# Recommender forward pass on one core: PSUM copies moved to VectorE, more table tiles fetched row by row from SP and ScalarE

## The chip, the cores and the metric

The kernel runs on one core of one Trainium2 chip. The metric is the device time in microseconds (us); the time of a kernel is the median of its runs. In the profile PE is TensorE's matmuls, PEld its weight loads, DVE is VectorE, ACT is ScalarE, POOL is GpSimd and SP is SyncE.

## The reference

A recommender model with attention over a user's history, for B = 16384 users, each with F = 69 item ids; the table `emb` has 100001 rows of E = 96 floats.

```python
u = emb[batch_user]                        # B x 69 x 96
ql = emb[batch_label[:, 0]]                # B x 96
q = broadcast(ql)
z = concatenate([q, u, q - u, q * u])      # B x 69 x 384
h = dice(z @ W1 + b1)                      # 64 wide
att = (h @ W2 + b2) @ W3 + b3              # one weight per item
pre = where(batch_user < ITEM_NUM, u * att, 0)
pooled = einsum('gf,bfe->bge', window, pre)   # 10 groups of items
x = concatenate([pooled, ql])
h = dice(bn(x @ Wf1 + bf1)); h = dice(bn(h @ Wf2 + bf2))
return h @ Wf3 + bf3
```

The items of a user fall into ten groups, and `dice(x) = (alpha * (1 - p) + p) * x` with `p = sigmoid(x)`. Everything is float32.

## The kernel before

**Tiling.** The users are cut into 32 blocks of 512. Of the 69 items of a block, the first 64 make 64 "main" chunks (8 users x 64 items each) and the last 5 make 5 "tail" chunks (512 users, one item each). A chunk is 512 rows of the table, fetched as 4 tiles of 128 rows. There are 32 x 69 = 2208 chunks, and two chunks make one step: 1104 steps, with up to 8 tiles per step.

**How a tile is fetched.** Most tiles are gathered by GpSimd with one indirect DMA of 128 rows (`gather`, L266) into the buffer `u` of the step. Some tiles, always the fourth of a chunk (`SLOT = 3`), are instead fetched row by row: 128 plain DMAs of one row (384 bytes) each, issued from SP's or ScalarE's own queue (L301, in `Singles.fetch`), into one of a few buffers of a tensor called `ring`. The byte offset of each row comes from a register; a register load (L286, in `Singles.load`) fetches the offsets of up to 32 rows from the tile `offsets`. `SP_CHUNKS` and `ACT_CHUNKS` list which chunks have such a tile: before, 109 tiles from SP (one every ten steps, in a ring of 4 buffers) and 136 from ScalarE (one every eight steps, in a ring of 3). SP has nothing else to do but loads and stores, so it runs ahead until its ring is full. ScalarE's rows are dealt out over the steps by the table `turn`: 16 rows per step in three pieces, one ahead of the step's fetch, one between its two chunks and one after it (`scalar_rows`), among ScalarE's other work.

**What a step does.** `fetch` (L359 on) takes for each of its two chunks a PSUM buffer `ptr` (two in all), transposes the four tiles into it on TensorE (L325), has VectorE multiply it by the query to give `quT` (L377, L384 for tail chunks), and has ScalarE copy it to `uT` (L386). `hidden` runs two steps later: four accumulating products per chunk pair into `ph` (L399, L403; two PSUM buffers), then on ScalarE a sigmoid (L405) and a scaled copy (L406), then on VectorE the product `y` (L407). `attend_rows` and `spread`, once per four steps, turn `y` into attention weights `rw` (L414, ScalarE's copy L416, L431, VectorE's L436). `pool` runs seven steps after the fetch: it multiplies the rows in `u` and `ring` by `rw` into `acc` (L325 again, since both go through the helper `read_rows`), and VectorE copies the sums to `pooled` (L470). After that the `u` buffer is free again; the pool of `u` has 14 buffers. For each block `head_gather`, `head_turn` (VectorE's copy L340) and `head_rows` (ScalarE's L349) prepare the query, and `top_steps` computes the dense layers (L502, with ScalarE's pair L483 and L484, called the dice pair below).

**What sets the order.** The order is written out by hand: `plan` lists the work of each of the 1104 steps, and each engine executes its own instructions in that order, waiting on semaphores. A tile of SP's list is placed in the plan six steps ahead of its use; SP may issue it earlier than that. A tile of ScalarE's list for step `m // 2` is dealt out over the `ACT_STEPS` steps that end three steps ahead of its use:

```python
for k in range(ACT_STEPS):
    turn.setdefault(m // 2 - 2 - ACT_STEPS + k, []).append((s, k * ACT_ROWS, min(P, (k + 1) * ACT_ROWS)))
```

Within a step the order is: tail work of step i - 3, `hidden` of step i - 2, `pool` of step i - 7, `fetch` of step i, then work of the blocks.

Of the kernel before, what the change touches and what calls it, by code (L numbers as in the profile page):

```python
# [19 lines left out]
B, F, E, G = 16384, 69, 96, 10  # L20
# [28 lines left out]

ROW_BYTES = 4 * E  # L50
SLOT = 3
SP_CHUNKS = [2 * (10 * s + 8) + 1 for s in range(109)]
SP_RING = 4
ACT_CHUNKS = [2 * (8 * s + 11) for s in range(136)]
ACT_RING = 3
ACT_ROWS = 16
ACT_STEPS = -(-P // ACT_ROWS)
SINGLES = SP_CHUNKS + ACT_CHUNKS
NSB = (len(SINGLES) + P - 1) // P
# [3 lines left out]
def chunk_of(c):  # L63

    n, k = divmod(c, NCH)
    if n == NBLK - 1 and k >= EARLY:
        k = NMAIN + k - EARLY if k < EARLY + NTAIL else k - NTAIL
    return n, k
# [47 lines left out]
def rec_kernel(  # L116
# [12 lines left out]
    nc = tc.nc  # L129
# [1 line left out]

    const = ctx.enter_context(tc.tile_pool(name="const", bufs=1))
    ipool = ctx.enter_context(tc.tile_pool(name="ipool", bufs=2))
    upool = ctx.enter_context(tc.tile_pool(name="upool", bufs=14))
    tpool = ctx.enter_context(tc.tile_pool(name="tpool", bufs=4))
    ypool = ctx.enter_context(tc.tile_pool(name="ypool", bufs=6))
    rpool = ctx.enter_context(tc.tile_pool(name="rpool", bufs=2))
# [3 lines left out]
    def by_field(ap):  # L141

        return ap.rearrange("e (s o) -> e s o", o=1).to_broadcast([ap.shape[0], NS, FM])
# [121 lines left out]
    def gather(table, dst, index):  # L265
        nc.gpsimd.indirect_dma_start(  # L266
            out=dst,
            out_offset=None,
            in_=table,
            in_offset=bass.IndirectOffsetOnAxis(ap=index, axis=0),  # L270
        )
# [3 lines left out]
    class Singles:  # L275
# [19 lines left out]
        def fetch(self, s, start, stop):  # L295

            b, k = self.buffers[s % len(self.buffers)], s % NSEM
            for r in range(start, stop):
                if r % self.group == 0:
                    self.load(s, r)  # L300
                d = self.engine.dma_start(  # L301
                    out=ring[r : r + 1, b], in_=row_bytes[:, bass.ds(self.values[r], ROW_BYTES)]
                ).then_inc(self.sems[k], 16)
                tc.no_tile_sem_insts.add(d.ins.name)
                tc.declare_no_dep(d.ins, group=f"ring{b}", reason="a buffer's readers have waited for its rows")
                fresh.setdefault(b, []).append(d.ins)
            if stop == P:
                for ins in fresh.pop(b):
                    tc.add_to_no_dep_group(f"ring{b}", ins)
                self.given[k] += 16 * P  # L310
                places[self.chunks[s]] = b, self.sems[k], self.given[k]
# [3 lines left out]
    def single(c, t):  # L315
        return places.get(c) if t == SLOT else None

    def wait_for_single(c, t):
        if single(c, t):
            nc.tensor.wait_ge(*single(c, t)[1:])  # L320

    def read_rows(op, out, u, c, t, other, **how):

        at = single(c, t)
        ins = op(out, ring[:, at[0]].bitcast(F32) if at else u[:, 4 * (c % 2) + t, :], other, **how)  # L325
        if at:
            tc.declare_no_dep(ins.ins, group=f"ring{at[0]}", reason="waited for by semaphore")
# [25 lines left out]
    def room(k):  # L353

        v = k % 4 if k < NMAIN else turns.index(min(turns))
        turns[v] += 1
        return uTs[v][turns[v] % len(uTs[v])]

    def fetch(i, between=None):  # L359

        u = upool.tile([P, 8, E], F32, tag="u", name=f"u{i}")
        uT = []
        quT = tpool.tile([E, 2, 512], F32, tag="quT", name=f"quT{i}")
        for j in range(2):
            if j == 1 and between:
                between()
            n, k = chunk_of(2 * i + j)
            ptr = ps_tr.tile([E, 512], F32, tag="tr", name=f"ptr{i}_{j}")
            for t in range(4):
                if single(2 * i + j, t):  # L370
                    wait_for_single(2 * i + j, t)
                else:
                    gather(rows, u[:, 4 * j + t, :], ids[n][:, 4 * k + t : 4 * k + t + 1])
                read_rows(nc.tensor.transpose, ptr[:, t * P : (t + 1) * P], u, 2 * i + j, t, ident)
            q = qTs[n % 2][0:E]
            if k < NMAIN:
                nc.vector.tensor_tensor(  # L377
                    quT[:, j, :].rearrange("e (s f) -> e s f", f=FM),
                    ptr.rearrange("e (s f) -> e s f", f=FM),
                    by_field(q[:, k * NS : (k + 1) * NS]),  # L380
                    ALU.mult,
                )
            else:
                nc.vector.tensor_tensor(quT[:, j, :], ptr, q[:, 0:BLK], ALU.mult)  # L384
            uT.append(room(k))
            nc.scalar.copy(uT[j][0:E], ptr)  # L386
        return u, uT, quT

    def hidden(i, uT, quT):
# [168 lines left out]
    def rows_of(b, n):  # L558
        return lambda: attend_rows(b, n)

    def spread_of(b, n):
        return lambda: spread(b, n)

    def pool_of(k):
        return lambda: pool(k)

    def hidden_of(k):
        return lambda: ys.__setitem__(k, hidden(k, *hs[k]))

    def tails_of(k):  # L570
        def work():
            uT = hs.pop(k)[0]
            for j in range(2):
                if chunk_of(2 * k + j)[1] >= NMAIN:
                    attend_tail(k, j, ys[k], uT)

        return work

    def fetch_of(k, between=()):
        def work():  # L580
            for j in range(2):
                n = chunk_of(2 * k + j)[0]
                if n not in pooled:
                    pooled[n] = bpool.tile([E, G, BLK], F32, tag="pooled", name=f"pooled{n}")
                    pres[n] = xpool.tile([E, NTAIL, BLK], F32, tag="pre", name=f"pre{n}")
            u, uT, quT = fetch(k, lambda: [w() for w in between])
            us[k], hs[k] = u, (uT, quT)

        return work
# [4 lines left out]
    def at(step, *work):  # L594
        plan.setdefault(step, []).extend(work)

    by_sync = Singles("sp", nc.sync, mybir.EngineType.SP, SP_CHUNKS, 0, range(SP_RING), 32)
    for s, m in enumerate(SP_CHUNKS):
        at(max(0, m // 2 - 6), lambda s=s: by_sync.fetch(s, 0, P))

    by_scalar = Singles(
        "act",
        nc.scalar,
        mybir.EngineType.Activation,
        ACT_CHUNKS,
        len(SP_CHUNKS),
        range(SP_RING, SP_RING + ACT_RING),
        2 * ACT_ROWS,
    )
    turn = {}  # L610
    for s, m in enumerate(ACT_CHUNKS):
        for k in range(ACT_STEPS):
            turn.setdefault(m // 2 - 2 - ACT_STEPS + k, []).append((s, k * ACT_ROWS, min(P, (k + 1) * ACT_ROWS)))

    def scalar_rows(i, third):

        for s, start, stop in turn.get(i, []):
            by_scalar.fetch(s, start + third * ACT_ROWS // 3, start + (third + 1) * ACT_ROWS // 3)

    c = NPAIR - CLOSE  # L620
    for i in range(c):
        if i >= 3 and (i - 3) % 4 == 3:
            at(i, rows_of(i - 6, 4))
        if i >= 3:
            at(i, tails_of(i - 3))
        if i >= 4 and (i - 4) % 4 == 3:
            at(i, spread_of(i - 7, 4))
        if i >= 2:
            at(i, hidden_of(i - 2))
        at(i, lambda i=i: scalar_rows(i, 0))  # L630
        if i < c - CLOSE:
            if i >= POOL_LAG:
                at(i, pool_of(i - POOL_LAG))
        else:

            for k in {0: (-15, -14), 1: (-13,), 3: (-12, -11), 4: (-10, -9), 7: (-8, -7)}.get(i - c + 8, ()):
                at(i, pool_of(c + k))
        at(i, fetch_of(i, [lambda i=i: scalar_rows(i, 1)]))
        at(i, lambda i=i: scalar_rows(i, 2))

    at(c, pool_of(c - 6), pool_of(c - 5), tails_of(c - 3), hidden_of(c - 2), fetch_of(c))
    at(c + 1, tails_of(c - 2), hidden_of(c - 1), fetch_of(c + 1))
# [113 lines left out]
```

## Time and profile before

| | before |
|---|---|
| median of 3 runs | 10951.15 us (10948.08 to 10951.86) |
| profiled execution: time / span | 10926.21 us / 10924.5 us |
| busy PE, PEld, DVE, ACT, POOL | 82%, 40%, 27%, 29%, 75% |
| mean granted TensorE clock | 0.739 of full speed |
| gathers issued by GpSimd | 8587 (rows) + 128 (queries) |
| rows issued one by one, ScalarE / SP | 17408 / 13952 |
| DMA engines, mean busy share | about 0.2 |

Busy time counts an engine's data instructions. Register loads, branches, semaphore instructions and the issuing of DMAs are not counted as busy, so an engine that issues many DMAs is more occupied than its busy share tells; such work stands under names ending in q (SPq, ACTq). A group's row gives the line, the engine, the operation, the tiles, the count, the busy time in us and the mean of one in ns, and then the idle time of the engine just before these instructions with the releasers that ended it.

### The profile page before, as it was taken

The numbers are of one execution on the slowest core, as the hardware profiler recorded it, in microseconds if no ns is written. First come the engines' busy times: TensorE is split into PE (matmuls) and PEld (weight loads), VectorE is DVE, ScalarE is ACT, GpSimd is POOL, SyncE is SP. The second block draws the span as 40 slices with busy tenths as digits, with TensorE's granted clock in tenths as the row PEclk, the third lists the DMA queues.
The fourth block names the chain that finished last, engine by engine and source line by source line (L and its number), as shares of the span: only waits on it lengthen the run. The fifth ranks groups of instructions, "written<-read, shape, count | busy, mean of one in ns | idle before, by whom it ended". The sixth has DMA issues, their size and how long they took to land.

```text
span 10924.5 us, 172151 instructions
## 1 busy us (share of the span) xinstructions
PE 8916.8 (82%) x41797; PEld 4347.4 (40%) x41797; DVE 2997.8 (27%) x5327; ACT 3181.0 (29%) x4969; POOL 8225.3 (75%) x8721
## 2 busy tenths in 40 slices
PE   7888888888887888888888878888788887888888
PEld 3343433334443343333443334433344343443335
DVE  3222222222222222222222222222222222222222
ACT  2222222222222222222222222222222222222223
POOL 7777777777777777777777777777777777777776
PEclk7767777677777777777777777777777777777777
DMA  2222222222222222222222222222222222222221
GB/s 50 42 41 44 42 42 41 42 44 41 42 42 42 44 41 42 42 41 44 42 42 41 41 44 42 42 42 42 44 42 42 41 42 44 42 41 42 42 41 35
DMA packets 344467, 458.51 MB, mean 42 GB/s; under 512 B 202354, under 2 KB 202866, under 8 KB 343330
## 3 DMA queue, kind: packets, MB, share of 16 engines
q0 software_dynamic: 278880, 428.92, 19.7%
q1 hardware_dynamic: 29762, 11.82, 0.5%
q10 hardware_dynamic: 34816, 6.75, 0.4%
q8 instruction: 336, 5.51, 0.2%
q14 instruction: 673, 5.51, 0.2%
HBM read 446.74 MB, written 0.07 MB: 41 GB/s over the span
## 4 chain that ended last, share of the span: by engine, by line
POOL 51%; issue 23%; PE 15%; DMA 9%; ACT 1%; DVE 0%; ACTq 0%; POOLq 0%; DVEq 0%
POOL u L266 50%; DMA u<-in_rows,ids 9%; PE p L502 4%; PE acc L325 3%; PE ph L403 2%; PE ph L399 2%; PE ptr L325 2%; POOL q L266 1%; PE prow L414 1%; PE ph L396 0%; PE ph L401 0%; PE pa L423 0%; PE pc L348 0%; PE patt L431 0%; ACTq L301 0%
## 5 line engine op out<-in xcount | busy, mean ns | idle before, releaser
L266 POOL DMA_INDIRECT u<-in_rows,ids x8587 | 8103.7, 944 | 2619.7 <-issue 2455.0
L325 PE MATMUL ptr<-ident,u 128*96 128x128 f32 x8587 | 2023.1, 335 | 1896.4 <-DMA u<-in_rows,ids 1864.9
L386 ACT COPY uT<-ptr 96x512 f32<-96x512 f32 x2208 | 1283.4, 581 | 4630.3 <-DVE quT L377 2969.4
L325 PEld LDWEIGHTS ptr<-ident,u 128*96 128x96 f32 x8587 | 1151.9, 150 | 2667.1 <-DMA u<-in_rows,ids 2224.0
L325 PEld LDWEIGHTS acc<-rw,u 128*96 128x96 f32 x15930 | 1696.6, 188 | 1209.0 <-issue 1018.4
L407 DVE TENSOR_TENSOR y<-ph,y 128x512 f32<-128x512 f32 x1104 | 763.0, 691 | 4981.9 <-ACT y L406 4704.9
L325 PE MATMUL acc<-rw,u 128*96 128x20 f32 x15930 | 1812.3, 259 | 52.0 <-DVE rw L436 41.9
L377 DVE TENSOR_TENSOR quT<-ptr,qT 96x512 f32<-96x512 f32 x2048 | 1368.6, 677 | 1737.7 <-PE ptr L325 1734.9
L399 PE MATMUL ph<-uT,A 128*64 128x512 f32 x4096 | 1651.8, 883 | 0.4 <-ACT uT L386 0.4
L403 PE MATMUL ph<-quT,wn 96*64 96x512 f32 x4416 | 1598.2, 794 | 0.0
L405 ACT ACTIVATE y<-ph 128x512 f32<-128x512 f32 x1104 | 658.5, 596 | 2401.0 <-PE ph L403 2283.5
L406 ACT ACTIVATE y<-y,wn,na1c 128x512 f32<-128x512 f32 x1104 | 898.2, 814 | 36.7
L403 PEld LDWEIGHTS ph<-quT,wn 96*64 96x64 f32 x4416 | 440.1, 188 | 1042.3 <-issue 1041.8
L502 PE MATMUL p<-pooled,wf 96*100 96x512 f32 (+1 forms) x1400 | 675.0, 630 | 0.0
L399 PEld LDWEIGHTS ph<-uT,A 128*64 128x64 f32 x4096 | 264.9, 176 | 615.6 <-issue 609.1
L414 PE MATMUL prow<-y,v 128*32 128x512 f32 x2208 | 465.2, 912 | 2.6 <-DVE y L407 2.6
L470 DVE COPY pooled<-acc 96x160 f32<-96x160 f32 x1008 | 420.3, 417 | 128.9 <-PE acc L325 128.8
L502 PE MATMUL p<-pre,V 96*100 96x512 f32 (+1 forms) x700 | 395.0, 710 | 2.9 <-DVE x L485 2.5
L502 PEld LDWEIGHTS p<-pooled,wf 96*100 96x100 f32 x1400 | 253.4, 193 | 322.6 <-issue 322.6
L436 DVE SCALAR_TENSOR_TENSOR rw<-patt,bb,wn 128x320 f32<-128x320 f32 x554 | 277.5, 542 | 216.1 <-PE patt L431 214.7
L416 ACT COPY row<-prow 128x512 f32<-128x512 f32 (+1 forms) x277 | 161.6, 583 | 413.1 <-PE prow L414 305.4
L431 PE MATMUL patt<-ident,row 128*128 128x128 f32 x1108 | 220.1, 334 | 17.3 <-DVE pre L424 15.6
(72 smaller groups left out, 2457.3 us busy)
## 6 DMA issues: line engine op xcount, KB each, us to landing
ring<-in_rows ACTq DMA_DIRECT2D x17408, 0.4 KB
ring<-in_rows SPq DMA_DIRECT2D x13952, 0.4 KB
u<-in_rows,ids POOLq DMA_INDIRECT x8587
ids<-in_idx SPq DMA_DIRECT2D x8, 560.0 KB, 3.9
q<-in_emb,ids POOLq DMA_INDIRECT x128
wf<-in_far SPq DMA_DIRECT2D x1, 1209.0 KB, 6.0
wn<-in_near SPq DMA_DIRECT2D x1, 236.0 KB, 3.4
ids<-in_idx SPq DMA_DIRECT2D x1, 140.0 KB, 2.2
```

The source lines that it names most:

```text
L266: nc.gpsimd.indirect_dma_start(out=dst, out_offset=None, in_=table, in_offset=bass.IndirectOffsetOnAxis(ap=index, axis=0),)
L325: ins = op(out, ring[:, at[0]].bitcast(F32) if at else u[:, 4 * (c % 2) + t, :], other, **how)
L377: nc.vector.tensor_tensor(quT[:, j, :].rearrange("e (s f) -> e s f", f=FM), ptr.rearrange("e (s f) -> e s f", f=FM), by_field(q[:, k * NS ...
L386: nc.scalar.copy(uT[j][0:E], ptr)
L399: nc.tensor.matmul(p, As[n % 2][:, k // 4, :], uT[j], start=True, stop=False)
L403: nc.tensor.matmul(p, Wp, quT[:, j, :], start=False, stop=True)
L405: nc.scalar.activation(y, ph, AF.Sigmoid, scale=S_DICE)
L406: nc.scalar.activation(y, y, AF.Identity, bias=a1c, scale=na1c)
L407: nc.vector.tensor_mul(y, ph, y)
L414: nc.tensor.matmul(pr[32 * k : 32 * (k + 1), :], v2, ys[b + k], start=True, stop=True)
L470: nc.vector.tensor_copy(pooled[n][:, :, k * NS : (k + 2) * NS].rearrange("e g s -> e s g"), pa.rearrange("e j s g -> e (j s) g"),)
L502: nc.tensor.matmul(p1, w[:, h * DH : (h + 1) * DH], x, start=(k == 0), stop=(k == KTOP - 1))
```

## The change

VectorE, instead of ScalarE, copies `ptr` to `uT`, ahead of its product for `quT`. ScalarE fetches 22 rows per step in one piece, with one register load per piece, so that a tile takes six steps (five of 22 rows and one of 18), and it serves 181 tiles, one every six steps. SP serves 199 tiles, one every five and a half steps, in a ring of 5 buffers. The pool of `u` has 13 buffers instead of 14.

```diff
-SP_CHUNKS = [2 * (10 * s + 8) + 1 for s in range(109)]
-SP_RING = 4
-ACT_CHUNKS = [2 * (8 * s + 11) for s in range(136)]
+SP_CHUNKS = [2 * (int(5.5 * s) + 6) + 1 for s in range(199)]
+SP_RING = 5
+ACT_CHUNKS = [2 * (6 * s + 9) for s in range(181)]
 ACT_RING = 3
-ACT_ROWS = 16
+ACT_ROWS = 22
 ACT_STEPS = -(-P // ACT_ROWS)
...
-    upool = ctx.enter_context(tc.tile_pool(name="upool", bufs=14))
+    upool = ctx.enter_context(tc.tile_pool(name="upool", bufs=13))
...
                 read_rows(nc.tensor.transpose, ptr[:, t * P : (t + 1) * P], u, 2 * i + j, t, ident)
+            uT.append(room(k))
+            nc.vector.tensor_copy(uT[j][0:E], ptr)
             q = qTs[n % 2][0:E]
...
                 nc.vector.tensor_tensor(quT[:, j, :], ptr, q[:, 0:BLK], ALU.mult)
-            uT.append(room(k))
-            nc.scalar.copy(uT[j][0:E], ptr)
         return u, uT, quT
...
         range(SP_RING, SP_RING + ACT_RING),
-        2 * ACT_ROWS,
+        ACT_ROWS,
     )
...
-    def scalar_rows(i, third):
+    def scalar_rows(i):
 
         for s, start, stop in turn.get(i, []):
-            by_scalar.fetch(s, start + third * ACT_ROWS // 3, start + (third + 1) * ACT_ROWS // 3)
+            by_scalar.fetch(s, start, stop)
...
-        at(i, lambda i=i: scalar_rows(i, 0))
+        at(i, lambda i=i: scalar_rows(i))
...
-        at(i, fetch_of(i, [lambda i=i: scalar_rows(i, 1)]))
-        at(i, lambda i=i: scalar_rows(i, 2))
+        at(i, fetch_of(i))
```

In the changed kernel VectorE's copy is line 376 and its product line 379. Per step, ScalarE's program is now: its copy L416 where there is one, the sigmoid L405, the scaled copy L406, one register load, 22 (or 18) row DMAs.

## The prediction

> **What bounds the kernel now.** I read the page first (busy time, then the costliest groups), then each engine's waits, then the timeline of one step of ScalarE.
>
> ```profile
> span 10924.5 us, 172151 instructions
> ...
> PE 8916.8 (82%) x41797; PEld 4347.4 (40%) x41797; DVE 2997.8 (27%) x5327; ACT 3181.0 (29%) x4969; POOL 8225.3 (75%) x8721
> ...
> L266 POOL DMA_INDIRECT u<-in_rows,ids x8587 | 8103.7, 944 | 2619.7 <-issue 2455.0
> L386 ACT COPY uT<-ptr 96x512 f32<-96x512 f32 x2208 | 1283.4, 581 | 4630.3 <-DVE quT L377 2969.4
> ...
> ring<-in_rows ACTq DMA_DIRECT2D x17408, 0.4 KB
> ring<-in_rows SPq DMA_DIRECT2D x13952, 0.4 KB
> ```
>
> PE has the largest busy share, but it is not the bound. GpSimd's 75% is. Its waits show why:
>
> ```profile
> POOL u L266 <- issue: 2455.0, 8047, 0.3
> POOL u L266 <- PE ptr L325: 56.1, 184, 0.3
> ```
>
> The last column is the longest wait: 0.3 us, so GpSimd never stops. Each gather takes 0.944 us and the next begins 0.3 us later. The first starts at 3.26 us, the last ends at 10886.3 us, and between them lie 8587 + 128 = 8715 gathers: 10883 / 8715 = **1.2488 us per gather**. A step (two chunks, 1104 in all) costs 10883 / 1104 = 9.86 us. After the last gather comes a tail of 38 us. Only fewer gathers can shorten this. The row-by-row tiles exist to do that, and what they cost is sequencer time on SP and ACT, which the busy line does not count. SP's own waits:
>
> ```profile
> SPq L301 <- PE ptr L325: 3594.1, 74, 95.2
> SPq L301 <- PE acc L325: 1286.1, 25, 97.6
> SPq L530 <- DVE r L529: 447.5, 1, 447.5
> ```
>
> SP is idle 5328 us and works about 5580, which is **0.40 us per row** (13952 rows), loads included. For the register loads I ask for the tile of offsets:
>
> ```profile
> L286 ACTq TENSOR_LOAD <-offsets x544: 2123/2182/2230, 21.5 to 10733.4; - x182
> L286 SPq TENSOR_LOAD <-offsets x436: 2052/2174/2397, 4.8 to 10449.9; - x146
> ```
>
> One load fetches 32 offsets and takes 2.18 us (min/median/max in ns). On ACT's timeline:
>
> ```profile
> 5361.23 0.81 ACT L406 ACTIVATE y<-y,wn,na1c 128x512 f32<-128x512 f32 x1
> 5361.30 1.43 ACTq L301 DMA_DIRECT2D ring<-in_rows  x5
> ...
> 5368.71 0.81 ACT L406 ACTIVATE y<-y,wn,na1c 128x512 f32<-128x512 f32 x1
> 5371.04 1.05 ACTq L301 DMA_DIRECT2D ring<-in_rows  x3
> ```
>
> Rows begin 0.07 us after the activation starts, or 2.33 us after it when a load stands between: issuing runs beside the activation, the load does too. Five rows in 1.43 us, the last 0.213 long, are 0.304 us apart.
>
> [...] the trace has only 32-value loads (2.18 us)[...]; the trace's own row is used instead:
>
> ```profile
> L340 DVE COPY qT<-pq 96x512 f32<-96x512 f32 x32 | 21.9, 686 | 6.5 <-PE pq L339 6.5
> ```
>
> [...]the gathers under the SBUF copies of L187 are longer:
>
> ```profile
> 11.70 4.23 DVE L187 COPY uT<-ident 32x512 f32<-32x512 f32 x12
> ```
> ```profile
> 12.16 1.12 POOL L266 DMA_INDIRECT u<-in_rows,ids  x1 [0.30 <-issue]
> ```
>
> **The change, part by part.**
>
> *Gathers.* Row-by-row tiles go from 109 + 136 = 245 to 199 + 181 = 380, so 135 gathers go: 135 x 1.2488 = **168.6 us** off GpSimd. New pace: 8580 x 1.2488 / 1104 = 9.705 us per step.
>
> *SP.* 199 x 128 = 25472 rows at 0.40 are 10190 us, from 7 us on. A tile takes 51.2 us and is wanted every 5.5 x 9.705 = 53.4. The first is wanted in step 6, at about 78 us, and is there at about 60; the lead grows by 2 us per tile until the five buffers stop it. Cover: 4%. The ids load that now follows the first tile is not needed before step 20. SP's waits shrink to a few hundred us and the cost on the path is nothing; with the cover gone, each 0.01 us per row is 255 us.
>
> *VectorE.* 2208 copies x 0.686 = 1515 us, so 4512 us busy of 10756, or 42%. They lie beside the gathers. A ptr buffer comes free 1.36 us after its transposes (copy, then product), where it waited for ACT's copy before; PE's waits on that copy were 52 us in all. Nothing on the path. If PSUM copies lengthened gathers they would cost; 31 gathers lie under the PSUM copies of L340 and average 0.943 us against 0.944 for all others, so I take zero, with a fall excluded.
>
> *ACT.* The copies go (1283 us). 181 x 128 = 23168 rows now come in 6 pieces per tile, 22 rows (the last 18), each with its own load: 1086 loads instead of 544. Everything in the piece stands ahead of the next sigmoid (L405), for which VectorE's L407 waits, with the accumulator copy and the copies of ptr behind it, and then PE for its two ph and two ptr buffers. ACT's sequencer per step: sigmoid to second activation 0.630; load to first row 0.125; first row to second 0.547 (so after every load in the trace); 20 more rows at 0.316 (their mean spacing while SP issues too) 6.32; last row to next sigmoid 0.26. Sum 7.88, less 4 rows in every sixth step 7.67. Beside it L416 (277 x 0.48), the dice pairs (105 x 1.44), L349 (64 x 0.58) and a second wait on each sigmoid: 0.32 per step. Together **7.99 us plus the load**, which is unmeasured at 22 values. In proportion it is 1.50 us[...]; unchanged 2.18. Averaged with the 18-row pieces: 1.46, 1.64, 2.18. ACT then needs **9.45, 9.63 or 10.17 us** per step against 9.705. I take the middle, since a load of one value can hardly cost a 32nd. A late ACT costs nothing by itself: PE runs a step behind, ph then always has work for ACT, and GpSimd can run five steps ahead with 13 u buffers (six with 14). Only the mean counts.
>
> *u buffers 14 to 13.* Nothing: GpSimd's longest wait is 0.3 us. If PE fell over five steps behind, that would show first as a GpSimd wait on acc.
>
> Sum: 10924.5 - 168.6 = 10755.9 us of span. The profiled execution took 10926.2 and the median of the runs is 24.9 above that, so the run time is 10926.2 - 168.6 + 24.9 = 10782.5; with a few us for ACT catching up, **10785 us**.
>
> **Rivals.**
>
> *ACT sets the pace, mildly.* For: 0.08 us of room in 9.7 is 1%. At 9.79 us per step over 1088 steps it costs 92 us: about 10875. Against: the load would have to take 1.80[...].
>
> *ACT sets the pace and loses.* The break-even is the old 9.86 us per step, a mean load of 1.87. A load that does not shrink gives (10.17 - 9.705) x 1088 = 506 us: about 11290. For: nothing shows how it scales.[...]
>
> *SP sets the pace.* From 0.417 us per row; slower than before from 0.424. At 0.44, 25472 rows end at 11215 us and the run takes about 11350. Against: SP's spacing is 0.330 whether ACT issues or not.
>
> *VectorE's copies hold up gathers.* At the start's 0.15 us, 2208 x 0.15 = 331: about 11115. Against: the L340 rows above.
>
> **How the numbers follow.** GpSimd keeps the pace 0.62; ACT mildly 0.17; a step within 0.02 us of the old 0.04; ACT loses 0.10; SP 0.04; copies against gathers 0.03. About 0.2% (22 us) is what a measurement of this kernel can tell from no change. Faster 0.62 + 0.17 = 0.79, same 0.04, slower 0.10 + 0.04 + 0.03 = 0.17. The range runs from 10770 (a shorter tail) to 10940, which takes in the mild case and leaves out the losing ones.
>
> **What would show it.** Right: L266 x8452 at 944 ns, its longest wait still 0.3 us; SP waiting a few hundred us; L376 x2208 near 686 ns; ACT's load at 1.5 to 1.7 us. Wrong: GpSimd waiting on acc for microseconds (PE late), then either the load near 2 us (ACT), or PE waiting on ring semaphores from SP; or gathers above 944 ns.

## The result, and the profile after

The change makes the kernel slower: median 12664.35 us (12657.51 to 12677.53) against 10949.61 us before, a ratio of 1.1569 with a 95% interval of 1.1555 to 1.1584. The forecast was 10785 us, so not only its size was wrong but its sign. The granted TensorE clock does not explain it: it was 0.745 in the changed kernel's profile and 0.739 in that of before.

The page of the changed kernel, its span, busy time, the chain of work that ended last by engine and by line, and three of its groups:

```profile
span 12675.8 us, 207661 instructions
...
PE 8803.0 (69%) x41797; PEld 4528.6 (36%) x41797; DVE 4165.9 (33%) x7535; ACT 1871.4 (15%) x2761; POOL 8119.0 (64%) x8586
...
ACTq 63%; ACT 13%; issue 13%; PE 10%; DVE 1%; POOL 0%; DMA 0%; DVEq 0%
ACTq L301 43%; ACTq L286 20%; ACT y L406 7%; ACT y L405 5%; PE acc L325 2%; PE ph L399 2%; PE ph L403 2%; PE prow L414 1%; PE ptr L325 1%; PE p L502 1%; PE pa L423 1%; ACT g L483 1%; ACT g L484 0%; DVE y L407 0%; PE ph L396 0%
...
L266 POOL DMA_INDIRECT u<-in_rows,ids x8452 | 7996.9, 946 | 4434.6 <-issue 2317.9
...
L405 ACT ACTIVATE y<-ph 128x512 f32<-128x512 f32 x1104 | 659.1, 597 | 7482.5 <-issue 5293.4
...
L376 DVE COPY uT<-ptr 96x512 f32<-96x512 f32 x2208 | 1480.1, 670 | 37.4 <-PE ptr L325 37.3
```

Every engine is busy for a smaller share than before except VectorE. ScalarE's busy share is the lowest of all, 15%, and yet the chain runs through it: ACTq, its sequencer, holds 63% of the span, 43% in row DMAs (L301) and 20% in register loads (L286). Before, GpSimd (POOL) held half of it:

```profile
POOL 51%; issue 23%; PE 15%; DMA 9%; ACT 1%; DVE 0%; ACTq 0%; POOLq 0%; DVEq 0%
```

GpSimd does have its 135 gathers fewer, at nearly the old duration (946 ns against 944). What is new is that it waits:

```profile
POOL u L266 <- issue: 2317.9, 7588, 0.6
POOL u L266 <- PE ptr L325: 1490.4, 473, 19.5
POOL u L266 <- PE acc L325: 541.4, 113, 18.1
```

The longest wait was 0.3 us before and is 19.5 us now, for TensorE. What a gather needs from TensorE is a free `u` buffer, and the last to read one is `pool` (acc). The view puts most of these waits down to the transposes (ptr), which follow `pool` in TensorE's order; that they are waits for `pool` is read from the kernel and not from the view. Below it stands the reason, in the view of the tile of offsets (min/median/max in ns):

```profile
L286 ACTq TENSOR_LOAD <-offsets x1086: 1844/2980/5132, 14.8 to 12483.9; - x181
L286 SPq TENSOR_LOAD <-offsets x796: 2030/2175/2477, 5.0 to 12359.1; - x199
```

ScalarE's loads fetch 22 offsets instead of 32 and take a median of 2.98 us instead of 2.18, with a spread from 1.84 to 5.13; SP's loads of 32 are as before. The timeline of ScalarE for two steps shows both kinds:

```profile
6016.45 0.81 ACT L406 ACTIVATE y<-y,wn,na1c 128x512 f32<-128x512 f32 x1
6018.53 6.91 ACTq L301 DMA_DIRECT2D ring<-in_rows  x22
6025.54 0.60 ACT L405 ACTIVATE y<-ph 128x512 f32<-128x512 f32 x1 [8.28 <-issue]
6026.17 0.81 ACT L406 ACTIVATE y<-y,wn,na1c 128x512 f32<-128x512 f32 x1
6031.38 7.34 ACTq L301 DMA_DIRECT2D ring<-in_rows  x22
6038.83 0.60 ACT L405 ACTIVATE y<-ph 128x512 f32<-128x512 f32 x1 [11.84 <-issue]
```

From the second activation to the first row pass 2.08 us in one step and 5.21 us in the next. The load itself, in each of the two steps:

```profile
L286 ACTq TENSOR_LOAD <-offsets x1: 1952/1952/1952, 6016.5 to 6016.5; - x1
```
```profile
L286 ACTq TENSOR_LOAD <-offsets x1: 5085/5085/5085, 6026.2 to 6026.2; - x1
```

Sorted by the piece of the tile, the medians over all 181 tiles are:

| piece | first column | its byte | values | median us |
|---|---|---|---|---|
| 1 | 0 | 0 | 22 | 1.90 |
| 2 | 22 | 88 | 22 | 5.05 |
| 3 | 44 | 176 | 22 | 1.90 |
| 4 | 66 | 264 | 22 | 5.06 |
| 5 | 88 | 352 | 22 | 1.91 |
| 6 | 110 | 440 | 18 | 4.18 |

Short and long loads alternate: the short ones begin at a multiple of 16 bytes in the tile's row, the long ones 8 bytes off. Two long sizes give (5.05 - 4.18) / 4 = 0.2175 us per value and 0.27 us at the start. The short loads fit 0.239 us for four values (32: 0.27 + 8 x 0.239 = 2.18; 22: 0.27 + 5 x 0.239 + 2 x 0.2175 = 1.90). That was the theory with which the experiments began.

### The profile page after: what moved, and what is told of

Read it like the earlier page. It is cut to its first block, busy times and chain, and to the rows that moved or that the text cites. A ratio compares the mean times of both kernels' runs of the same rounds, so it can differ in the third digit from the quotient of the medians.

```text
span 12675.8 us, 207661 instructions
## 1 busy us (share of the span) xinstructions
PE 8803.0 (69%) x41797; PEld 4528.6 (36%) x41797; DVE 4165.9 (33%) x7535; ACT 1871.4 (15%) x2761; POOL 8119.0 (64%) x8586
## 4 chain that ended last, share of the span: by engine, by line
ACTq 63%; ACT 13%; issue 13%; PE 10%; DVE 1%; POOL 0%; DMA 0%; DVEq 0%
ACTq L301 43%; ACTq L286 20%; ACT y L406 7%; ACT y L405 5%; PE acc L325 2%; PE ph L399 2%; PE ph L403 2%; PE prow L414 1%; PE ptr L325 1%; PE p L502 1%; PE pa L423 1%; ACT g L483 1%; ACT g L484 0%; DVE y L407 0%; PE ph L396 0%
## 5 line engine op out<-in xcount | busy, mean ns | idle before, releaser
L266 POOL DMA_INDIRECT u<-in_rows,ids x8452 | 7996.9, 946 | 4434.6 <-issue 2317.9
L325 PE MATMUL acc<-rw,u 128*96 128x20 f32 x15672 | 1895.3, 267 | 1443.6 <-DVE pooled L470 807.8
L325 PEld LDWEIGHTS acc<-rw,u 128*96 128x96 f32 x15672 | 1775.6, 198 | 2519.3 <-DVE pooled L470 1164.2
L325 PE MATMUL ptr<-ident,u 128*96 128x128 f32 x8452 | 1597.0, 340 | 343.6 <-issue 264.1
L405 ACT ACTIVATE y<-ph 128x512 f32<-128x512 f32 x1104 | 659.1, 597 | 7482.5 <-issue 5293.4
L414 PE MATMUL prow<-y,v 128*32 128x512 f32 x2208 | 836.7, 882 | 1323.6 <-DVE y L407 1170.4
L399 PE MATMUL ph<-uT,A 128*64 128x512 f32 x4096 | 1566.5, 840 | 0.0
L376 DVE COPY uT<-ptr 96x512 f32<-96x512 f32 x2208 | 1480.1, 670 | 37.4 <-PE ptr L325 37.3
L403 PE MATMUL ph<-quT,wn 96*64 96x512 f32 x4416 | 1447.3, 723 | 0.0
L325 PEld LDWEIGHTS ptr<-ident,u 128*96 128x96 f32 x8452 | 1221.7, 166 | 524.5 <-issue 342.8
L406 ACT ACTIVATE y<-y,wn,na1c 128x512 f32<-128x512 f32 x1104 | 897.4, 813 | 37.2
L414 PEld LDWEIGHTS prow<-y,v 128*32 128x32 f32 x2208 | 91.0, 130 | 1757.3 <-DVE y L407 1479.3
L416 ACT COPY row<-prow 128x512 f32<-128x512 f32 (+1 forms) x277 | 161.8, 584 | 2031.4 <-PE ptr L325 1142.7
```

The lines of the kernel that those rows point to most:

```text
L266: nc.gpsimd.indirect_dma_start(out=dst, out_offset=None, in_=table, in_offset=bass.IndirectOffsetOnAxis(ap=index, axis=0),)
L376: nc.vector.tensor_copy(uT[j][0:E], ptr)
L399: nc.tensor.matmul(p, As[n % 2][:, k // 4, :], uT[j], start=True, stop=False)
L403: nc.tensor.matmul(p, Wp, quT[:, j, :], start=False, stop=True)
L405: nc.scalar.activation(y, ph, AF.Sigmoid, scale=S_DICE)
L406: nc.scalar.activation(y, y, AF.Identity, bias=a1c, scale=na1c)
```

## The experiments

**Theory A**: a load that begins off a 16-byte boundary takes 0.2175 us for every value (5.05 us for 22), one that begins on it 0.239 us for every four (1.90 us for 22), and the loads off the boundary made ScalarE the bound. Where the expectation of e1 says that registers are fetched one by one or four at a time, that is my reading of these times; the traces show the times alone. **Theory B**: loads grew because SP loads at the same time, or because of the odd size. **Theory C**: 22 rows in one piece ahead of the sigmoid hold up VectorE and TensorE whatever the load takes. The first four kernels ran together on one chip where before takes 10925.6 us, the last four on another where it takes 10947.6 us; each is compared with before on its own chip. The 8486 us in the expectations is the time of ScalarE's sequencer in the changed kernel without its loads, taken from its trace in the way told with the last table below.

**e1_padded.** The offsets of ScalarE's tiles are laid out 24 columns per piece, in rows of 144:

```diff
+WIDE = 144
+def column(piece, r):
+    return r if piece == 32 else 24 * (r // piece) + r % piece + 0
...
-                offsets[i % P : i % P + 1, i // P, start:stop],
+                offsets[i % P : i % P + 1, i // P, column(self.group, start) : column(self.group, stop - 1) + 1],
```

> The changed kernel, with ScalarE's offsets laid out 24 columns per piece instead of 22, so that every load begins at a multiple of four columns (16 bytes); rows, pieces and loads are as many as in the changed kernel. Theory A (a load that begins off a 16-byte boundary fetches its registers one by one, about 0.22 us each; one that begins on it fetches four at a time, about 0.24 us): all loads of 22 take 1.90 us and those of 18 about 1.66, mean 1.86 instead of 3.31. ScalarE's sequencer then has 8486 + 1086 x 1.92 = 10570 us of work, under GpSimd's 10756, so the time falls to 10790 to 11100 us, likeliest 10830. Theory B (loads got longer because SP loads at the same time, or because 22 is an odd size): loads stay at a mean near 3.3 us and the time stays near 12660. Theory C (22 rows in one piece ahead of the sigmoid hold up VectorE and TensorE, whatever the load takes): loads shorten, but the time falls by less than half of the 1880 us to the expected value, to above 11700.

Measured: 11150.9 us, ratio 1.0204 (1.0187 to 1.0221). The load (line 291 here) and the chain by engine:

```profile
L291 ACTq TENSOR_LOAD <-offsets x1086: 1627/1890/1958, 16.8 to 10967.7; - x181
```
```profile
ACTq 55%; ACT 14%; issue 14%; PE 13%; DVE 2%; POOL 1%; DMA 0%; POOLq 0%
```

Every load is fast now, 1.89 us, mean 1.865. Where the loads begin is worth 1513 us (12664 - 11151), or some 1490 if the 24 us by which before is faster on this chip are taken off. B is out, and C with it as the main cause. But the kernel is still 2% slower than before, 50 us above the expected range, and the chain still runs through ScalarE. Theory A's claim that work below GpSimd's pace is enough is not right.

**e2_all_off.** As e1, with `+ 2` in place of `+ 0`: every load begins 8 bytes off.

> As the kernel with 24 columns per piece, but all of ScalarE's columns moved by two, so that every one of its loads begins 8 bytes off a 16-byte boundary. Theory A: every load of 22 takes 5.05 us and of 18 4.18, mean 4.91, which is 1.60 us more than in the changed kernel; ScalarE bound, 1086 x 1.60 = 1730 us more: about 14400 us. Theory B: loads as in the changed kernel, about 12660. Theory C: load times of no weight, within 300 us of 12660.

Measured: 14246.82 us, ratio 1.3038 (1.3016 to 1.3059).

```profile
L291 ACTq TENSOR_LOAD <-offsets x1086: 4017/4942/5121, 16.5 to 14062.7; - x181
```

The time is some 150 us below the expected 14400. Together with e1 and the changed kernel there are now three sizes of the same cause: mean loads of 1.865, 3.31 and 4.86 us give 11151, 12664 and 14247 us. Both intervals have about the same slope, 1046 and 1023 us of run time per us of load, where 1086 loads all on the path would give 1086.

**e3_rows24.** One number:

```diff
-ACT_ROWS = 22
+ACT_ROWS = 24
```

> The changed kernel with ACT_ROWS = 24 instead of 22: a tile still takes six steps (five of 24 rows and one of 8), and every piece begins at a multiple of four columns without padding. Theory A: loads of 24 take 0.27 + 6 x 0.239 = 1.70 us, of 8 0.75 us, mean 1.54; ScalarE's sequencer has 8486 + 1086 x 1.60 = 10220 us of work against GpSimd's 10756: 10785 to 10850 us, faster than before. Theory B: near 12600. Theory C: longer pieces, so no better than with 22 rows, 12600 or more.

Measured: 10891.64 us, ratio 0.9972 (0.9959 to 0.9984): faster than before, by less than expected.

```profile
L286 ACTq TENSOR_LOAD <-offsets x1086: 711/1677/1737, 15.4 to 10714.9; - x181
```
```profile
L266 POOL DMA_INDIRECT u<-in_rows,ids x8452 | 7980.3, 944 | 2682.7 <-issue 2397.2 <-PE ptr L325 118.5 <-DMA u<-in_rows,ids 116.1
```

The loads take what theory A said, and pieces that are longer by two rows are no harm, against theory C. GpSimd still waits: beyond its usual 1.249 us from gather to gather it loses some 105 us.

**e4_loads.** The kernel before, with SP's loads cut into pieces of many sizes:

```diff
+PIECES = [1, 2, 3, 4, 5, 6, 7, 8, 12, 16, 20, 22, 22]
+PIECES2 = [2, 16, 22, 24, 32, 18, 8, 4, 1, 1]
...
-                if r % self.group == 0:
+                if (r == 0 or r in stops(s)) if self.name == "sp" else r % self.group == 0:
```

> The kernel before, with SP's register loads cut into pieces of 1 to 32 values that begin at many columns (SP idles half of the span there, so the time should stay within 0.5% of before). Theory A: a load that begins at a multiple of four columns takes 0.27 + 0.239 per four values + 0.2175 per value left over (4: 0.51, 8: 0.75, 16: 1.23, 24: 1.70, 32: 2.18, 18: 1.66, 22: 1.90); any other takes 0.27 + 0.2175 per value (1: 0.49, 8: 2.0, 16: 3.75, 22: 5.05), and whether it is off by one, two or three columns makes no difference. Theory B: SP's loads depend on their size alone.

Measured: one run, 10929.27 us, as before. Medians of the 1255 loads by size and first column, in us:

```
values  begins at a multiple of 4 columns   begins elsewhere
 1      0.52                                0.54 (off by 2), 0.50 (off by 3)
 2      0.74                                0.71 (off by 1)
 8      0.80                                1.98 (off by 2)
12      1.03                                -
16      1.26                                3.63 (off by 2)
18      1.69                                -
20      1.49                                -
22      1.93                                4.88 (off by 2)
24      1.72                                -
32      2.19                                -
 3      -                                   0.94 (off by 3)
 4      -                                   1.15 (off by 2)
 5      -                                   1.36 (off by 2)
 6      -                                   1.56 (off by 3)
 7      -                                   1.77 (off by 1)
```

The rule of theory A holds within 8% (10% for one of the single values, 0.54 us against 0.49), on SP as on ScalarE, for starts that are off by one, two or three columns. 24 values cost less than 22, and 22 from a wrong column cost more than twice 32.

**e5_group32.** The changed kernel, with loads of 32 again, at rows 0, 32, 64 and 96 of a tile, wherever these fall in the pieces of 22 rows:

```diff
         range(SP_RING, SP_RING + ACT_RING),
-        ACT_ROWS,
+        32,
     )
```

> The changed kernel with ScalarE's offsets loaded 32 at a time again (at rows 0, 32, 64 and 96 of a tile, so sometimes in the middle of a piece of 22 rows); everything else as changed. Theory A (the start columns of the loads made the change slow): 724 loads of 2.18 us instead of 1086 of 3.31; with 0.30 us per load that stands around it, ScalarE has 8486 - 362 x 0.30 + 724 x 2.24 = 10000 us of work, 7% under GpSimd's 10756. The time is 10760 to 10850 us, GpSimd's waits beyond 0.3 us sum to under 60 us, and the change as a whole would have been faster than before. Theory C (22 rows ahead of the sigmoid hold things up): above 11300. A mixed theory (ScalarE's work plus some 0.4 us per step that it waits on TensorE sets the pace): 10000 + 500 + 150 of start and tail = 10650, under GpSimd's pace, so as theory A.

Measured: 10805.07 us, ratio 0.9873 (0.9856 to 0.9889).

```profile
L286 ACTq TENSOR_LOAD <-offsets x724: 2110/2279/2522, 16.6 to 10612.8; - x181
```
```profile
POOL u L266 <- issue: 2420.9, 7899, 2.4
POOL u L266 <- DMA u<-in_rows,ids: 111.3, 317, 1.2
POOL u L266 <- PE ptr L325: 43.6, 134, 1.2
```
```profile
ACTq 30%; POOL 23%; issue 17%; PE 14%; DMA 10%; ACT 5%; DVE 1%; POOLq 0%
```

GpSimd's longest wait is 2.4 us. What its gaps exceed the usual 1.252 us by sums to some 22 to 30 us, depending on how it is counted, nearly all in the first 3000 us. The chain is shared between ScalarE's sequencer and GpSimd. The 22 rows still stand in one piece ahead of the sigmoid, so theory C falls. There are also 362 loads fewer than in e1, so this run does not part their start from their number; e1 and e2 do. This is the fastest kernel of the study, ahead of before and of the changed kernel.

**e6_sp_only.** The kernel before with `SP_CHUNKS`, `SP_RING = 5` and 13 `u` buffers of the change.

> The kernel before with SP's part of the change alone: 199 tiles from SP, its ring of 5 buffers and 13 u buffers; ScalarE's rows and copies as before. 90 gathers fewer at 1.2488 us. If neither SP's rate nor the 13 u buffers bind: 112 us less than before, about 10815 on a chip where before takes 10926, gathers of 944 ns and no wait of GpSimd above 0.3 us. If SP binds (rows above 0.417 us): TensorE waits on SP's semaphores and the time is above 10926.

Measured: 10838.03 us, ratio 0.9899 (0.9882 to 0.9915): 110 us less, where 112 were expected. GpSimd's longest wait stays at 0.3 us, and SP is left with a wait of some 360 us for its ring:

```profile
POOL u L266 <- issue: 2397.3, 7850, 0.3
```
```profile
SPq L301 <- PE ptr L325: 312.5, 79, 11.3
SPq L301 <- PE acc L325: 50.3, 10, 9.4
```

**e7_copy_only.** The kernel before with the copies on VectorE, ahead of the product; nothing else.

> The kernel before with the copies of ptr moved to VectorE alone; rows, pieces and loads as before. If VectorE's copies lie beside the gathers: within 15 us of before, 2208 copies of 670 to 690 ns, gathers still 944 ns. If they hold up gathers or TensorE's ptr buffers: GpSimd waits over 0.3 us or gathers above 944 ns, and up to 330 us more.

Measured: 10947.35 us, ratio 1.0 (0.9991 to 1.0009), and the copies as priced:

```profile
L376 DVE COPY uT<-ptr 96x512 f32<-96x512 f32 x2208 | 1493.5, 676 | 1461.2 <-PE ptr L325 1458.3
```
```profile
L266 POOL DMA_INDIRECT u<-in_rows,ids x8587 | 8123.6, 946 | 2621.4 <-issue 2401.5 <-DMA u<-in_rows,ids 138.4 <-PE ptr L325 61.7
```

The gathers take 946 ns and not the expected 944. The copies are not the reason: in e6, on the same chip and with the copies still on ScalarE, they take 946 ns too. GpSimd's longest wait for a `u` buffer stays at 0.3 us.

**e8_act_copies.** As e5, with the copies back on ScalarE:

```diff
-            uT.append(room(k))
-            nc.vector.tensor_copy(uT[j][0:E], ptr)
...
+            uT.append(room(k))
+            nc.scalar.copy(uT[j][0:E], ptr)
```

> The changed kernel with loads of 32 and with the copies of ptr back on ScalarE (after VectorE's product, as before). If the move of the copies is what makes room for 22 rows: two copies per step stand in line on ScalarE and each waits for VectorE, some 1.2 us per step, 10000 + 1325 = 11325 us of work and waits: 11300 to 11900 us. If the move was of no weight: as with VectorE's copies, about 10800.

Measured: 11637.42 us, ratio 1.0629 (1.0611 to 1.0647). The copy stands at the end of 22 rows in ScalarE's order, and TensorE waits 2.7 ms for it in sum:

```profile
L325 PE MATMUL ptr<-ident,u 128*96 128x128 f32 x8452 | 1769.2, 370 | 2725.5 <-ACT uT L386 2702.2
```

So the move of the copies, which alone is worth nothing (e7), is worth 832 us beside 22 rows in one piece.

## Why the prediction was wrong, point by point

**What held.** The bound before and the price of a gather: SP's 90 tiles alone brought 110 of 112 us (e6). SP's rate, its cover and the 13 buffers (e6: GpSimd's longest wait 0.3 us, SP's for its ring some 360 us in sum). VectorE's copies: 676 ns against 686, no cost (10947.35 us against 10947.6), no effect on gathers (946 ns in e7 and in e6). The rival that ScalarE's load decides, and that a load mean above 1.87 us means slower, was named; it was given 0.10.

**The step that failed.** It is the price of the register load at 22 values, in the part on ScalarE (ACT). The prediction bounded it by 1.50 and 2.18 us (means 1.46 to 2.18) and took 1.64, an estimate of my own that no trace had shown; it measured a mean of 3.31, above the upper bound. The upper bound rested on the argument that a smaller load cannot cost more than a larger one, which was an assumption: all 980 loads of the kernel before fetched 32 values and began at columns 0, 32, 64 and 96, so its trace could show neither what another size costs nor what another start costs. The diff did show that the start would change, from multiples of 32 to multiples of 22. I read it for the number of values alone. The middle guess was too low for good starts as well: e1's mean is 1.865 us, where the fit has 0.2175 us for each of the two values left over after the groups of four, and against 1.64 that alone is some 245 us over 1088 steps. Its reason, that one value costs more than a 32nd of 32 values, held: 0.50 to 0.54 us against 2.19 (e4).

**How much this explains.** The prediction's own sum, 7.99 us plus the load, gives 7.99 + 3.31 = 11.30 us per step with the measured load. The span gives (12676 - 193) / 1088 = 11.47, if the last 16 steps (16 x 9.7) and the tail of 38 us go as forecast. The difference is 0.17 us per step. That it is so small is in part luck: over 1088 steps the sum gives 12294 us, more than all the work in the table below (12152), and it has no term for the 524 us of waiting. The 1879 us between forecast and result split by e1 into 1513 us for the columns and some 366 that remain.

**The second step that failed** is the sentence "Only the mean counts". In e1 the mean load was 1.865 us, below the break-even of 1.87; the forecast's sum would put the time at that of before, and it came out 225 us above. Walking through ScalarE's sequencer in the trace, and counting as waiting what exceeds the usual spacing of two instructions and as work all the rest of the span, gives:

| kernel | work us | waiting us | sum (the span) | run time us |
|---|---|---|---|---|
| changed | 12152 | 524 | 12676 | 12664 |
| e1_padded | 10616 | 536 | 11152 | 11151 |
| e3_rows24 | 10264 | 633 | 10897 | 10892 |
| e5_group32 | 10108 | 696 | 10804 | 10805 |

(Counting only the waits ahead of ScalarE's computing instructions makes the waiting 80 to 100 us smaller in each.) Work in e1 was close to the 10570 us expected, and under GpSimd's 10750 to 10800 us. But ScalarE also waits some 0.5 us per step, mostly ahead of the sigmoid, for TensorE. The product that the next sigmoid needs stands in TensorE's order behind work that waits for VectorE, and VectorE's product `y` waits for ScalarE's scaled copy (7423 us in sum in the changed kernel). TensorE's waits there show the other half:

```profile
PE prow L414 <- DVE y L407: 1170.4, 221, 9.1
PE acc L325 <- DVE pooled L470: 807.8, 313, 6.5
```

In the changed kernel's profile 10% of the chain is on PE, in e1 13%. So an engine whose work alone lay under GpSimd's pace still set the time in e1. In e5 GpSimd's gathers are on the chain again and TensorE waits 764 us in sum for gathered rows; ScalarE's 696 us can hold such waits too, so they don't tell what the round trip alone would cost. That this round trip causes the waiting is read from the chain and the waits; no run removed it by itself.

**The rival with the opposite sign.** Its mechanism, ScalarE's sequencer above 9.86 us per step, is what happened. Its price, about 11290, assumed a load that does not shrink, 2.18 us; the load grew, to a mean of 3.31.

**The change without the flaw.** With one number different (e5) the change gives 10805 us, 142.5 us less than before on that chip. The forecast's 168.6 us less would be 10779; the missing 26 us are about the size of GpSimd's gaps (22 to 30 us); closer than that it is not resolved.

## What to carry to other kernels

When a change alters a size, look at every address that the size sets, and ask whether the trace of before has ever seen such an address: here 2.18 us, measured for 32 values from multiples of 16 bytes, was no bound for 22 values from 8 bytes off, which took 5.05. An upper bound needs a reason of its own; "smaller cannot cost more" was none. An engine whose mean work was within a few per cent of the bound set the pace itself once its own waits in the loop were added (e1: 10616 us of work and 536 of waiting, with GpSimd's pace at 10750 to 10800), and an issuing sequencer must be counted by its register loads and row spacing, since the busy line shows ScalarE at 15% where its sequencer holds 63% of the chain.

## What the runs showed of the hardware that I had not expected

- In these runs a register load from SBUF took 0.27 us plus 0.239 us for each four values and 0.2175 us for each value left over if it began at a multiple of 16 bytes in the tile's row, and 0.27 us plus 0.2175 us for each value otherwise: 1.90 against 5.05 us for 22 values (changed kernel, e1, e2; e4 agrees within 4% at this size). Why is not shown.
- The gather's duration differed a little between the two chips: 944 ns in e1 to e3 on one, 946 in e5 to e7 on the other. The profile of before has 944 ns too. Over 8715 gathers, at 1.2488 us from start to start before and 1.2513 in e7, that is 22 us. That is also about the distance between the profiled execution of before (10926.21 us, 944 ns) and the median of its other runs (10949.61 us).
- In the changed kernel the row DMAs of the two sequencers hardly disturbed each other: SP's rows are on average 0.330 us apart where ScalarE issues none and 0.331 where it does, and ScalarE's 0.322 and 0.332 (spacings under 1 us).
